# A four-block transformer stack on one core: 768-column rows in block 4, a shared bank in linear attention, loads as a part, tiles reused at the end

## The chip, the core and the metric

The kernel runs on one core of one Trainium2 chip. The time is the device time of one execution, in microseconds. Before the change three runs gave a median of 2755.65 us (2754.45 to 2756.18). One further execution was recorded by the hardware profiler; it took 2750.45 us, and its instructions span 2748.6 us. All durations below are from that execution.

## The reference

The input `x` holds 8 sequences of 1024 rows of 256 numbers in fp32. Four blocks follow each other, each added to `x` and each behind a layernorm without gain (`ln` below):

```
x = x + decoder(ln(x))        # block 1: linear "flow" attention, 16 heads of 16, then
                              #   h = LN1(in + attn @ Wo + bo); LN2(h + gelu(h W1 + b1) W2 + b2), hidden 1024
x = x + relu(ln(x) w1 + b1) w2 + b2          # block 2: hidden 1024
x = x + softmax(q k^T / 16) v                # block 3: one head of 256, per sequence of 1024
x = x + fp4(silu(fp4(y) Wg^T) * (fp4(y) Wu^T)) Wd^T,  y = ln(x)   # block 4: hidden 704
```

In block 1 `q` and `k` are sigmoids; running sums over the rows of `q`, `k` and weighted `q`, `k` give for each row and head a scale for the query and one for the value, and `out = q_scaled @ cumsum(k^T v_scaled)`. In block 4 `fp4` quantises and restores blocks of 16 numbers along a row, for activations and for the weights (whose restored values are written `fp4(W)` in the reference).

## The kernel before

**Tiling.** Work goes by chunks of 128 rows (64 in all), and in block 1 by groups of four chunks (512 rows, 16 groups). TensorE products are fp32; each product in the code is two passes in the trace. Three producers run at once. `linear_attention` does block 1's attention group by group: `front` (load, layernorm, transpose) for four chunks, the q and k products, running sums on VectorE (`prod`), `head_sums`, a trip of a small table through HBM that spreads it over partitions (`packed`, `spread`), the same once more, and then `linear_chunk` four times: values, scores `k q` in 32-row tiles with masks (`sc`), the values product in 32-column tiles that also reads the carried state `kv_sum`, the state's increment `k^T v`, and the output product. `dense` does the two hidden-1024 layers in halves of a group and streams their weights (`w_ff`, five buffers, 128 KB loads) through the one DMA queue of SyncE. `softmax_and_fp4` starts `soft_chunk` for one chunk after another: scores against the whole sequence, exponentials, transposes, value product, then block 4. Two more parts, `fp4_weights` and `softmax_weights`, prepare weights at the start: the first loads the raw weights of block 4 (`w_raw`), quantises them with `fp4` on VectorE and ScalarE and transposes them; the second forms the product of the block-3 query and key weights from `wqk_raw`.

**Order.** The order of the instructions on each engine is fixed when the program is built. `Plan` runs the parts as generators. Each `yield` names an engine, the tiles that must be done, free buffers and PSUM banks, and a priority `at`. `Plan.run` (line 231) picks the part that can start first, and among those the one with the lowest `at`; `took` (line 140) adds an estimated duration for each instruction. The estimates decide the order only; on the chip each engine takes its instructions in that order and waits for what they need. All five engines are pinned to it, and DMAs are all issued by SyncE.

**Buffers.** `TILES` (line 42) gives each kind of working tile a number of buffers. `lin` has 5 (linear attention), `flow` 9, `soft` 5 and `prob` 7 (softmax and block 4), `rows` 4, `x` 4 and `hid` 3 rows of 704 columns. A chunk of block 3 and 4 starts only while fewer than 4 are unfinished, and its first product only while fewer than 2 wait for their values. PSUM has eight banks; `linear_chunk` takes one for the values product and another for `k^T v`.

**Start.** The constants (`rpos`, `same`, `front` among them) are computed on VectorE before anything else, and all biases, gains and small weights are loaded on the SyncE queue before the parts run: x for four chunks, the q, k, v weights, Wo and nine rows spread over the partitions, 128 KB each.

**The end of block 4.** A row of `hid` has 704 = 5 x 128 + 64 columns. `soft_chunk` transposes it tile by tile, copies five full tiles and one of 64 rows to `hqT`, and multiplies six tiles with `wdT`:

```
for k, (f0, rows_) in enumerate(INTER_TILES):
    nc.tensor.matmul(
        bank[:, :D],
        lhsT=hqT[k // 4][:rows_, k % 4, :],
        rhs=wdT[:rows_, k, :],
```

Of the kernel before, what the change touches and what calls it, by code (L numbers as in the profile page):

```python
# [33 lines left out]
BANKS = 8  # L34
INTER_TILES = [(t * P, min(P, INTER - t * P)) for t in range((INTER + P - 1) // P)]
# [9 lines left out]
    "lin": (5, D, F32),  # L45
# [7 lines left out]
    "hid": (3, INTER, F32),  # L53
    "q_c": (2, INTER, BF16),
}


class Plan:
# [9 lines left out]
    def __init__(self, tc, nc):  # L68
        self.tc, self.nc = tc, nc
        self.free = {}  # L70
        self.done = {}
        self.by = {}
        self.banks = []
        self.live = {}
        self.slots = {}
        self.kind = {}
        self.used = {}
        self.held = set()
        self.kept = set()
        self.last = {}  # L80
        self.act_set = 0
        self.parts = []
        for name in ("tensor", "vector", "scalar", "gpsimd", "sync"):
            setattr(self, name, Queue(self, name))
# [19 lines left out]
    def take(self, kind, tile_):  # L104
        name = tile_.tensor.name
        slots, live = self.slots.setdefault(kind, []), self.live.setdefault(kind, set())
        if len(live) + len(slots) == TILES[kind][0]:
# [11 lines left out]

    def slot_free(self, kind):  # L120
        slots, live = self.slots.get(kind, []), self.live.get(kind, ())
        if len(live) + len(slots) < TILES[kind][0]:
            return 0.0
        return min(slots) if slots else None

# [5 lines left out]

    def bank_free(self, tag, n, count):
        banks = self.banks.get(tag, [])
        if len(banks) + count <= n:
            return 0.0
        times = sorted(self.used[b] for b in banks if b not in self.held)
        k = count - (n - len(banks)) - 1
        return times[k] if k < len(times) else float("inf")

    def took(self, queue, op, args, kw):  # L140
# [12 lines left out]
        if queue == "tensor":  # L153
# [4 lines left out]
            if op == "matmul" and (kw["lhsT"].shape[-1] <= 32 or kw["lhsT"].shape[0] <= 32):  # L158
                cost *= 0.25
            after = 0.2  # L160
        elif queue == "vector":
            each = {"reciprocal": 6.2e-3, "tensor_tensor_scan": 2.15e-3}.get(op, 1.05e-3)
            cost = 0.15 + each * size
        elif queue == "scalar":
            cost = 0.2 + 0.95e-3 * size
# [4 lines left out]
        elif queue == "gpsimd":  # L170
            cost = 0.4 + 1.3e-3 * size
        else:
            cost, after = 0.4, 2.2
# [7 lines left out]
        end = start + cost  # L181
        self.free[queue] = end
# [11 lines left out]
    def need(queue, tiles, banks=0, when=None, at=None, unused=(), fresh=None):  # L194
# [3 lines left out]
            queue=queue, tiles=tiles, banks=banks, when=when, at=at, unused=unused, fresh=fresh  # L198
# [14 lines left out]
    def ready(self, need):  # L213
# [8 lines left out]
        if need.fresh is not None:  # L222
            times.append(self.slot_free(need.fresh))
# [7 lines left out]
    def run(self):  # L231
        while self.parts:
            now = self.free.get("tensor", 0.0)
            best = None
            for part in self.parts:
# [3 lines left out]
                key = max(t - now, 0.0), part[1].queue == "tensor", part[2]  # L239
                if best is None or key < best[0]:  # L240
                    best = key, part
            assert best is not None, "every part waits for another"
            if best[0][0] > 0.0:
                self.free["tensor"] = now + best[0][0]
# [42 lines left out]
def block_stack_kernel(ctx: ExitStack, tc: tile.TileContext, a: dict, out: bass.AP):  # L287
# [51 lines left out]
    def make(kind, name=None):  # L339
        bufs, width, dtype = TILES[kind]  # L340
        t = wk.tile([P, width], dtype, tag=kind, name=name or kind, bufs=bufs)
# [11 lines left out]
    def load_row(name, width):  # L353
        t = const.tile([P, width], F32, tag=f"b_{name}", name=f"b_{name}")
        nc.sync.dma_start(out=t, in_=a[name].partition_broadcast(P))
        return t

    def load_tiles(name, width, kt):
        t = const.tile([P, kt, width], F32, tag=f"w_{name}", name=f"w_{name}")
        nc.sync.dma_start(out=t, in_=a[name].rearrange("(k p) n -> p k n", p=P))  # L360
        return t

    def load_cols(name, n):
        t = const.tile([P, n], F32, tag=f"c_{name}", name=f"c_{name}")
        nc.sync.dma_start(out=t, in_=a[name])
        return t
# [32 lines left out]
    for g in range(NG):  # L399
        nc.vector.tensor_scalar(rpos[:, g, :], pos, float(g * GT), None, ALU.add)  # L400
    nc.vector.reciprocal(rpos, rpos)
# [16 lines left out]
    nc.vector.tensor_reduce(  # L418
        same[:, 0, :], ident.rearrange("p (t r) -> p r t", r=32), AX.X, ALU.add
    )  # L420
    front = const.tile([P, G, 32], F32, name="front")
    nc.vector.memset(front, 0.0)
    for t in range(1, G):
        nc.vector.tensor_copy(same[:, t, :], same[:, 0, :])
        nc.vector.tensor_copy(front[: 32 * t, t, :], same[: 32 * t, 0, :])
# [3 lines left out]
    for i in range(V_PADS):  # L429
        v = const.tile([P, H, 32], F32, name=f"v_pad{i}")  # L430
        nc.gpsimd.memset(v, 0.0)
        v_pads.append(v)

# [11 lines left out]
    for i, n in enumerate("qkv"):  # L445
        nc.sync.dma_start(
            out=wqkv[:, :, i * D : (i + 1) * D],
            in_=a[f"L0_attn_W{n}"].rearrange("(k p) n -> p k n", p=P),
        )
        if n != "v":  # L450
# [4 lines left out]
    bv1 = load_row("L0_attn_bv", D)  # L455
    wo = load_tiles("L0_attn_Wo", D, 2)
    bo = load_row("L0_attn_bo", D)
    ln1g, ln1b = load_row("L0_attn_ln1_g", D), load_row("L0_attn_ln1_b", D)
    b1 = load_cols("L0_attn_b1", NF)
    b2 = load_row("L0_attn_b2", D)  # L460
    ln2g, ln2b = load_row("L0_attn_ln2_g", D), load_row("L0_attn_ln2_b", D)
    fb1 = load_cols("L0_ffn_b1", NF)
    fb2 = load_row("L0_ffn_b2", D)
    wv3 = const.tile([P, 2, D], F32, name="wv3")
    nc.sync.dma_start(
        out=wv3, in_=a["L1_attn_W_qkv"][:, 2 * D :].rearrange("(k p) n -> p k n", p=P)
    )
    bsm = load_cols("L1_attn_b_qk", 4)
    bsv = load_row("L1_attn_b_v", D)
# [4 lines left out]
    wdT = const.tile([P, len(INTER_TILES), D], F32, name="wdT")  # L474

# [88 lines left out]
    def fp4_weights():  # L564
# [15 lines left out]
        for i, (src, turns) in enumerate(pieces):  # L580
            for j in range(i, min(i + 3, len(pieces))):
                if j not in raws:
                    ahead = pieces[j][0]
                    raws[j] = (yield from fresh("soft", dma(), "w_raw"))[
# [835 lines left out]
```

## Time and profile before

| | |
|---|---|
| median of 3 runs | 2755.65 us |
| profiled execution | 2750.45 us, span 2748.6 us |
| TensorE (PE) busy | 2614.9 us, 95% |
| TensorE weight loads (PEld) busy | 1998.1 us, 73% |
| VectorE (DVE) busy | 1953.3 us, 71% |
| ScalarE (ACT) busy | 1219.6 us, 44%, of it 285 activation table loads of 1.28 us |
| GpSimd (POOL) busy | 597.7 us, 22% |
| DMA | 211.61 MB, mean 77 GB/s |
| granted TensorE clock, mean | 0.984 |

A row of a group reads: line, engine, operation, output and inputs by name, shape of the tile in the array (rows*columns), operand shape, count, then busy time in us and the mean of one in ns, then the idle time of the engine just before these instructions with what ended it. As passes overlap, the mean of one is longer than the distance from one start to the next. A row of a timeline reads: start, duration, engine, operation and names; PEld is the load of weights into the array, SPq the issue of a DMA. Nearly all rows carry line 268, since one helper issues every instruction, so they are told apart by the names of their tiles. A waiting row reads: total us, times, longest.

### The profile page before, as it was taken

Reading aid. Unit: us, or ns where it says so; the run is one execution under the profiler, and the core shown is the slowest. Engines: PE = TensorE matmul, PEld = TensorE weight load, DVE = VectorE, ACT = ScalarE, POOL = GpSimd, SP = SyncE. Lnnn points to the kernel's source line nnn. Section 1 sums busy time; section 2 is a strip of 40 time slices with the busy share of each in tenths; the row PEclk is TensorE's granted clock in tenths of the full one; section 3 lists DMA queues with packets and bytes.
Section 4 is the critical chain, followed back from the end, with each engine's and each line's share of the span. In section 5 each row is a group of like instructions: output and inputs, shape, how many; then the busy total and the mean of one; then the engine's idle time right before and its main releaser. Section 6 shows DMA issues by size and latency. Waiting matters only on the chain.

```text
span 2748.6 us, 45646 instructions
## 1 busy us (share of the span) xinstructions
PE 2614.9 (95%) x16620; PEld 1998.1 (73%) x16620; DVE 1953.3 (71%) x4459; ACT 1219.6 (44%) x2453; POOL 597.7 (22%) x1100
## 2 busy tenths in 40 slices
PE   3888999999999999999999999999999999999997
PEld 1667677777777777777777777777777777877664
DVE  6877676685867778587776858768685777755565
ACT  2424344534554454444535354444545445353343
POOL 1323322121321312122221223213131222211000
PEclk7999999999999999999999999999999999999999
DMA  4234231322223232232222223222322313122000
GB/s 107 76 103 141 71 104 57 93 71 86 82 68 98 65 92 67 75 102 62 90 66 78 82 79 100 62 90 69 90 65 80 109 49 91 60 80 76 14 12 14
DMA packets 283215, 211.61 MB, mean 77 GB/s; under 512 B 23921, under 2 KB 270705, under 8 KB 282993
## 3 DMA queue, kind: packets, MB, share of 16 engines
q1 hardware_dynamic: 282992, 208.71, 25.5%
q8 instruction: 133, 2.18, 0.3%
q14 instruction: 90, 0.73, 0.1%
HBM read 189.74 MB, written 18.87 MB: 76 GB/s over the span
## 4 chain that ended last, share of the span: by engine, by line
PE 83%; DVE 11%; DMA 2%; ACT 2%; issue 1%; POOL 1%; SPq 0%; DVEq 0%; POOLq 0%; ACTq 0%
PE bank L268 83%; DVE hid L268 3%; DVE n L268 1%; DVE x_amax L268 1%; DVE ln_st L268 1%; DMA spread<-packed 1%; DVE mx L268 1%; DVE sc L268 1%; DVE prod L268 1%; ACT L268 1%; DMA w_ff<-in_L_ffn_w_dram 1%; SPq L268 0%; DVE u L268 0%; DVE x_r L268 0%; POOL ln_rstd L268 0%
## 5 line engine op out<-in xcount | busy, mean ns | idle before, releaser
L268 PE MATMUL bank<-half,w_ff 128*128 128x256 f32 x2048 | 533.8, 384 | 17.1 <-DMA w_ff<-in_L_ffn_w_dram 13.7
L268 PE MATMUL bank<-w_ff,hidden 128*128 128x256 f32 x2048 | 530.4, 384 | 3.4 <-ACT hidden L268 3.4
L268 PEld LDWEIGHTS bank<-half,w_ff 128*128 128x128 f32 x2048 | 382.8, 192 | 94.9 <-issue 32.3
L268 PEld LDWEIGHTS bank<-w_ff,hidden 128*128 128x128 f32 x2048 | 366.9, 191 | 76.4 <-issue 29.6
L268 ACT ACT_TABLE_LOAD x285 | 365.7, 1283 | 61.9 <-PE bank L268 54.6
L268 POOL TENSOR_SCALAR ln_ve<-ln_mv 128x1 f32<-128x1 f32 x384 | 102.4, 267 | 1110.1 <-DVE ln_mv L268 1099.6
L268 ACT ACTIVATE hidden<-bank,c_L_ffn_b 128x256 f32<-128x256 f32 x256 | 120.8, 472 | 320.5 <-PE bank L268 319.8
L268 PE MATMUL bank<-n2T,qT 128*128 128x512 f32 x512 | 243.9, 599 | 2.3 <-ACT qT L268 2.3
L268 POOL TENSOR_TENSOR ln_rstd<-ln_ve,neghalf 128x1 f32<-128x1 f32 x384 | 237.4, 618 | 32.0
L268 PE MATMUL bank<-vt,probT 128*128 128x256 f32 x1024 | 232.2, 380 | 0.0
L268 DVE TENSOR_TENSOR hid<-hid,bank 128x352 f32<-128x352 f32 x128 | 65.9, 518 | 229.4 <-PE bank L268 189.2
L268 PEld LDWEIGHTS bank<-vt,probT 128*128 128x128 f32 x1024 | 194.0, 190 | 38.1 <-issue 7.7
L268 DVE TENSOR_TENSOR sc<-bank,triu 128x512 f32<-128x512 f32 x256 | 162.3, 682 | 54.9 <-PE bank L268 54.9
L268 PE MATMUL bank<-wdT,hqT 128*128 128x256 f32 (+1 forms) x768 | 190.9, 390 | 0.8 <-ACT hqT L268 0.8
L268 ACT ACTIVATE hidden<-bank,c_L_attn_b 128x256 f32<-128x256 f32 x256 | 121.5, 474 | 146.3 <-PE bank L268 144.8
L268 POOL TENSOR_TENSOR xr<-xr,b_L_attn_ln_b 128x256 f32<-128x256 f32 x64 | 62.6, 996 | 531.3 <-DMA xr<-in_L_attn_inputs_dram 531.1
L268 PE MATMUL bank<-wgT,xqT 128*128 128x352 f32 x512 | 175.4, 465 | 1.4 <-ACT xqT L268 1.4
L268 PE MATMUL bank<-wuT,xqT 128*128 128x352 f32 x512 | 172.4, 459 | 0.0
L268 PEld LDWEIGHTS bank<-wdT,hqT 128*128 128x128 f32 (+1 forms) x768 | 139.7, 190 | 40.8 <-issue 20.2
L268 PEld LDWEIGHTS bank<-n2T,qT 128*128 128x128 f32 x512 | 92.7, 191 | 73.7 <-issue 62.5
L268 PEld LDWEIGHTS bank<-wuT,xqT 128*128 128x128 f32 x512 | 97.3, 190 | 54.1
L268 ACT ACTIVATE hid<-bank 128x352 f32<-128x352 f32 x128 | 59.3, 463 | 154.0 <-PE bank L268 152.6
(174 smaller groups left out, 4382.5 us busy)
## 6 DMA issues: line engine op xcount, KB each, us to landing
w_ff<-in_L_attn_W_dram SPq DMA_DIRECT2D x512, 128.0 KB
w_ff<-in_L_ffn_w_dram SPq DMA_DIRECT2D x512, 128.0 KB
spread<-packed SPq DMA_DIRECT2D x96, 256.0 KB
x<-in_L_attn_inputs_dram SPq DMA_DIRECT2D x64, 128.0 KB
xr<-in_L_attn_inputs_dram SPq DMA_DIRECT2D x64, 128.0 KB
rows<-res SPq DMA_DIRECT2D x64, 128.0 KB
rows<-rows SPq DMA_DIRECT2D x64, 128.0 KB
out_dram<-y SPq DMA_DIRECT2D x64, 128.0 KB
```

Source lines behind the costliest of these rows:

```text
L268: ins = method(*args, **kw)
```

## The change

- Block 4's rows are 768 wide. Three `hid` tiles are allocated once, with columns 704 to 767 set to zero, and so are the missing 64 rows of `wdT`. Transposes, the copy and the down product then use full 128-row tiles. The quantisation still covers 704 columns.
- In `linear_chunk`, the values product and `k^T v` share one bank; `start=False` for the second. `lin` has 4 buffers.
- Constants needed later (`rpos`, `same`, `front`) and most loads become parts, `late_constants` and `late_loads`, with priorities of their own; whoever reads them waits for a label in `late`. The preparation of the block-4 weights gets later priorities.
- When the last linear chunk is done, `plan.spare` lets `prob`, `soft` and `rows` also take `flow`, `lin` and `x` tiles, the tiles of `q` and `k` become two more `hid` rows, eight chunks may be unfinished in place of four, and three may wait for values in place of two.
- The planner's estimates change: TensorE pays 0.2 us when the array's shape changes, and a part that stays in 32-wide tiles is preferred; other constants for VectorE, ScalarE and GpSimd; a DMA takes its bytes at 160 GB/s, one behind another, and lands 1.8 us after.

```diff
-    "lin": (5, D, F32),
+    "lin": (4, D, F32),
-    "hid": (3, INTER, F32),
+    "hid": (3, INTER_PAD, F32),
+SPARE = {"prob": "flow", "soft": "lin", "rows": "x"}
...
+            tiled = op == "matmul" and (kw["lhsT"].shape[-1] <= 32 or kw["lhsT"].shape[0] <= 32)
+            if tiled:
                 cost *= 0.25
+            if tiled != self.tiled:
+                cost += 0.2
...
+            if op == "tensor_scalar" and outs[0].dtype == BF16:
+                cost = 0.16 + 0.26e-3 * size
         elif queue == "scalar":
-            cost = 0.2 + 0.95e-3 * size
+            cost = (0.16 if op == "copy" else 0.26) + 0.82e-3 * size
...
         elif queue == "gpsimd":
-            cost = 0.4 + 1.3e-3 * size
+            cost = 0.2 if op == "tensor_scalar" else 0.55 + 0.7e-3 * size
         else:
-            cost, after = 0.4, 2.2
+            cost = 0.4
...
+        if queue == "sync":
+            n = 4e-6 / 160e-3
+            for d in outs[0].shape:
+                n *= d
+            self.free["rings"] = max(self.free.get("rings", 0.0), end) + n
+            after = self.free["rings"] - end + 1.8
...
-                key = max(t - now, 0.0), part[1].queue == "tensor", part[2]
+                stays = self.tiled and part[1].tiled
+                wait = max(t - now - (0.3 if stays else 0.0), 0.0)
+                key = wait, part[1].queue == "tensor", not stays, part[2]
...
+    def late_loads():
+        loads.sort(key=lambda x: x[0])
+        for i, (at, label, t, src) in enumerate(loads):
+            yield dma(at=at)
+            nc.sync.dma_start(out=t, in_=src)
+            if all(x[1] != label for x in loads[i + 1 :]):
+                late.add(label)
...
-    for g in range(NG):
-        nc.vector.tensor_scalar(rpos[:, g, :], pos, float(g * GT), None, ALU.add)
-    nc.vector.reciprocal(rpos, rpos)
...
+    def late_constants():
+        yield dve(at=0.1)
+        for g in range(NG):
+            nc.vector.tensor_scalar(rpos[:, g, :], pos, float(g * GT), None, ALU.add)
+        nc.vector.reciprocal(rpos, rpos)
+        yield dve(at=0.12)
...
+    hids = []
+    for i in range(TILES["hid"][0]):
+        h = const.tile([P, INTER_PAD], F32, name=f"hid{i}")
+        nc.gpsimd.memset(h[:, INTER:], 0.0)
+        hids.append(h)
...
-            at = 0.2 + 2.5 * i / len(pieces)
+            at = 0.9 + 2.2 * i / len(pieces)
...
-        bank = mm_bank()[:, :D]
+        both = mm_bank()
+        plan.keep(both)
+        bank = both[:, :D]
...
-            kvbank = mm_bank()[:, :64].rearrange("p (k d) -> p k d", k=2)
+            kvbank = both[:, D : D + 64].rearrange("p (k d) -> p k d", k=2)
...
-                        start=k == 0,
+                        start=False,
...
+        yield pe(when=lambda: count["linear"] == B * NCH)
+        plan.spare = True
+        for n in ("q", "k"):
+            h = kept([P, 2, GT], n, 1).rearrange("p k t -> p (k t)")
+            nc.gpsimd.memset(h[:, INTER:INTER_PAD], 0.0)
+            hids.append(h[:, :INTER_PAD])
+        plan.size["hid"] += 2
...
-        yield pe(banks=1, when=lambda: count["asked"] == cc and count["asked"] - count["valued"] < 2)
+            and count["asked"] - count["valued"] < (3 if plan.spare else 2),
...
-            bank = tr_bank()
-            for k, (f0, rows_) in enumerate(tiles):
-                nc.tensor.transpose(bank[:rows_, k, :], hid[:, f0 : f0 + rows_], ident)
+            bank = turned([hid[:, f0 : f0 + P] for f0, _ in tiles])
...
+            nc.scalar.copy(hqT[half][:, : len(tiles), :], bank)
...
-                lhsT=hqT[k // 4][:rows_, k % 4, :],
-                rhs=wdT[:rows_, k, :],
+                lhsT=hqT[k // 4][:, k % 4, :],
+                rhs=wdT[:, k, :],
...
-                when=lambda: q["normed"] == NCH and cc - count["out"] < 4 and "softmax" in weights,
+                when=lambda: q["normed"] == NCH and cc - count["out"] < (8 if plan.spare else 4) and "softmax" in weights,
...
-    for part in (linear_attention(), dense(), softmax_and_fp4(), fp4_weights(), softmax_weights()):
+    for part in (linear_attention(), late_constants(), late_loads(), dense(), softmax_and_fp4(), fp4_weights(), softmax_weights()):
```

## The prediction

> **What bounds the kernel now.** I read the page's busy shares first, then the four stretches of the run by busy time, then the waits of TensorE, then the groups split by shape, and last the timelines of one block-4 product and of the first 46 us.
>
> ```profile
> PE 2614.9 (95%) x16620; PEld 1998.1 (73%) x16620; DVE 1953.3 (71%) x4459; ACT 1219.6 (44%) x2453; POOL 597.7 (22%) x1100
> ```
>
> TensorE is busy for 2614.9 of 2748.6 us, so 133.7 us are idle. The stretches (from:to, length, then busy time by engine, granted clock) show where:
>
> ```profile
> 0.00:100.00 100.00, 44.80 (x441) 30.54 (x445) 66.90 (x168) 22.36 (x58) 16.98 (x43) 0.81 0.31 83
> 100.00:420.00 320.00, 288.66 (x2041) 228.37 (x2037) 241.42 (x553) 131.79 (x285) 91.72 (x165) 0.95 0.36 106
> 420.00:2550.00 2130.00, 2116.23 (x13479) 1626.33 (x13468) 1525.68 (x3472) 991.99 (x1960) 479.90 (x875) 1.00 0.26 79
> 2550.00:2748.60 198.60, 165.18 (x681) 112.91 (x679) 119.26 (x267) 73.47 (x151) 9.07 (x18) 0.96 0.04 12
> ```
>
> Idle on TensorE: 55.2, 31.3, 13.8 and 33.4 us. For 2130 us it is the bound with nothing to spare, so there only less TensorE time counts. In the first 420 us and the last 200 us it waits for others; there an earlier start or more chunks in flight count.
>
> The longest waits of TensorE, totals over the run with count and longest, are of those two ends, and no engine starves it in between:
>
> ```profile
> PE bank L268 <- DVE prod L268: 20.7, 6, 7.8
> PE bank L268 <- DVE n L268: 16.6, 9, 11.3
> PE bank L268 <- DVE hid L268: 14.4, 5, 7.3
> PE bank L268 <- DMA w_ff<-in_L_ffn_w_dram: 13.7, 2, 7.2
> PE bank L268 <- DMA wqk_raw<-in_L_attn_W_qkv_dram: 8.4, 1, 8.4
> ```
>
> **Block 4 padded to 768 columns.** The last of six tiles of the down projection has 64 rows. By shape (count, busy, mean ns):
>
> ```profile
> L268 PE MATMUL bank<-wdT,hqT 128*128 128x256 f32 x640 | 150.8, 383 | 0.8 <-ACT hqT L268 0.8
> L268 PE MATMUL bank<-wdT,hqT 64*128 64x256 f32 x128 | 44.5, 428 | 0.0
> ```
>
> And one product in the steady part, with the rows of another that show the weight loads:
>
> ```profile
> 1320.24 2.02 PEld L268 LDWEIGHTS bank<-wdT,hqT 128*128 128x128 f32 x10 [0.20 <-issue]
> 1322.60 0.29 PEld L268 LDWEIGHTS bank<-wdT,hqT 64*128 64x128 f32 x2 [0.33 <-issue]
> 1323.22 0.89 PEld L268 LDWEIGHTS bank<-wgT,xqT 128*128 128x128 f32 x4 [0.33 <-issue]
> ...
> 1325.69 3.62 PE L268 MATMUL bank<-vt,probT 128*128 128x256 f32 x16
> 1329.15 1.05 PE L268 MATMUL bank<-wgT,xqT 128*128 128x352 f32 x3
> ...
> 1347.68 2.95 PE L268 MATMUL bank<-wdT,hqT 128*128 128x256 f32 x12
> 1350.56 0.44 PE L268 MATMUL bank<-ident,n 128*128 128x128 f32 x2
> ```
>
> The weight load stands idle for 0.33 us before the 64-row tile and again before the next full one: it is not overlapped with the product ahead. Sixteen full passes take 1329.15-1325.69 = 3.46 us, 0.216 each; twelve of them would take 2.59. The product takes 1350.56-1347.68 = 2.88. So 0.29 us a chunk x 64 chunks = **-18.4 us**, nearly all where TensorE is the bound. The page "TensorEngine Tiling (Array Packing)" of the Trainium skill speaks against this: its tables (Theoretical Speedup; Row Tiling) recommend a 64-row tile for a contraction of 64, with up to twice the rate. By that, the two last passes would take half of 2 x 0.216 now, and padding would lose 0.22 x 64 = 14 us. The row decides: the two passes lie alone between full tiles, with no second 64-row tile beside them, and pay both changes of shape. The transpose of the last 64 columns already streams 128 columns and stays. ScalarE writes one copy in place of two (about 0.15 us x 64): nothing, it is 44% busy. GpSimd gains four small memsets before its first layernorm work, under 1 us by its 0.52 us for a 512-column memset, hidden by VectorE, which gets to the normalisation later.
>
> **Order of tiled products.** The planner now charges a change of array shape and keeps 32-wide products together. Counted in the two instruction orders, changes fall from 294 to 280. A change costs about 0.09 us (the passes of 0.216 take 0.31 at a change): **-1.3**.
>
> **Late loads and constants.** Before, the first transposes run at 11.3 but the third normalisation is stuck on VectorE behind the quantisation of a block-4 weight that lands at 18.4, and TensorE's second half of the transposes behind W_qk:
>
> ```profile
> 18.42 0.42 DVE L268 TENSOR_REDUCE x_amax<-w_raw 128x16 f32<-128x256 f32 x1 [6.72 <-DMA w_raw<-in_L_ffn_w_gate_dram]
> 20.88 0.69 PE L268 MATMUL bank<-ident,wqk_raw 128*128 128x128 f32 x2 [8.44 <-DMA wqk_raw<-in_L_attn_W_qkv_dram]
> 33.85 1.22 DVE L268 TENSOR_TENSOR_SCAN prod<-one,k 128x512 f32<-128x512 f32 x1
> ```
>
> In the new order all four normalisations, then all transposes, then the first q/k products precede W_qk; rpos, same and front (about 4 us) move between and behind the statistics. But one weight's first four VectorE steps still stand before the first scan. Its transfer is the queue's 3072nd KB both before (x 512, four 256 KB weights, nine 128 KB rows, wv 256, itself 128) and after (x, the four weights, five rows, W_qk 512, one w_ff 256, itself). It lands at 18.4 again; four steps take 1.5 us, and the scan starts at 20.0 instead of 33.85. Its input is there by then: without rpos, same and front ahead of them the statistics start near 5.6, the four normalisations end near 13.0 (x and W_k, the queue's first 1024 KB, have landed by 8), and the first q/k product takes 3.3 us on the slow clock (23.49 to 26.79 before) and the sigmoid 0.7, so k is ready near 18. Without the weight in front the scan would gain 2 us more. The scan chain, the two trips through HBM (packed, spread) and the four chunks follow in nearly the same order, so the first dense product moves from 98.1 by 13.9. The queue behind it holds another 2560 KB, at 3072 KB in about 15.5 us until 31.3; the first packed row is sent at about 31.5, so 1 us may be lost: **-13** (bounds -5 and -18). The loads put behind W_qk and w_ff (norms, wv, its bias) have landed by 31.3 and are first read beyond 100 in the old run, near 90 in the new: the gap of some 55 us covers them; without it each 128 KB row would cost 0.6. Late next is the 256 KB spread of each flow.
>
> **Better costs of transfers and engines.** In 100 to 420 us the two waits for w_ff (13.7) follow a w_ff load issued behind 1 MB of spread. The planner now counts such backlog and may put other work there, but little other work exists yet. Between 0 and all of it, and 8 us the other way since the earlier start asks for weights sooner: I take **-6**.
>
> **One bank for values and k v.** VectorE's read of k v must now follow ScalarE's copy of xo, as the new waits show; before, 90.35 (kv) overlaps 90.18 (xo). The page "PSUM — Partial Sum Buffer" (PSUM bank collisions) asks for this guard by bank. Queued behind it on VectorE are the masks of the next scores. Uncovered it would cost a copy, 0.37 us x 56 = 20.7; by the rows the delay is 0.2 to 0.37 and the next reader of the sum has over 3.5 us of TensorE work before it. Only the first group has no cover: **+1**. One bank less in demand and one fewer `lin` tile (4, not 5): nothing; the new order leaves more TensorE work between scores and their use (lower quartile 5 to 6.4 us against 4.6 to 5).
>
> **Tiles reused for the last chunks.** Work on TensorE behind the last wv product is 146 us in both orders; before, this took 194. Behind the last qT product lie 26.4 us of work before (it took 47) and 35.0 after: 8.6 of idle filled. Of the other 17.8 us of idle since 2550 I take half, since eight chunks with three at the scores leave other work at each wait: **-17** (bounds -5, -26). The clock of 0.96 over 165 us of work costs 6.6; half goes: **-3**.
>
> **Sum.** -18.4-1.3-13-6+1-17-3 = -57.7 on the profiled execution's 2750.45 (span 2748.6 and 1.9 around it): 2692.7. The median of the runs lies 5.2 above that execution: **2698**.
>
> **Rivals.**
> - The early gain is taken back by the stalls in 100 to 420 us, since weights are asked for sooner and the transfers are no faster: +19, 2717. For: w_ff waits there already. Against: the chain of the second group moves forward too.
> - The tail stays bound by the latency of a chunk, its quantisation on VectorE (7.3 us wait in the last): only -3 of the -20, 2715. For: VectorE steps are the same. Against: idle is spread over many chunks.
> - More: early stalls down by 13 more and the tail by 10 more, 2675.
> - Slower: VectorE, waiting for xo behind an activation table load (1.28) and a hidden activation (0.47) on ScalarE, lets scores pile up and TensorE stall in each chunk: 1.75 x 56 = 98, 2796. It decides from 57.7/56 = 1.03 us a chunk. Against: 13.8 us idle in 2130, and 29% free on VectorE.
> - The new order does nothing net, about 2755: the planner's other choices cost what the steps gain. Nothing in the profile asks for it.
>
> **How the numbers follow.** All as stated 0.50 (own range 2685 to 2712), early gain lost 0.18, tail kept 0.15, more 0.09, same 0.03, slower 0.05. A run tells from no change what exceeds 0.2% (5.5 us). Faster 0.92, same 0.03, slower 0.05. Range 2672 to 2730: from the better case to past both partial losses.
>
> **What would show it.** Right: no 64-row group and 2.6 us a product; first scan near 20, first dense product near 85; idle after the last dense product under 20 us, clock there above 0.97; 420 to 2550 idle still under 1%. Wrong: waits for kv or w_ff growing, idle of the steady part above 30 us, or a first scan still past 30.

## The result

The changed kernel takes 2736.28 us (median of five runs, 2731.74 to 2747.50) against 2755.65 us before: a ratio of 0.994, with a 95% interval of 0.9922 to 0.9957. It is faster, by 19 us. The forecast was 2698 us, 58 us faster, and its range began at 2672 and ended at 2730, so the measured time lies outside. The direction was right and the size was not.

The profiled execution of the changed kernel took 2747.50 us, the longest of the five; a likely reason stands in the last section. TensorE's share on its page has hardly moved:

```profile
PE 2608.8 (95%) x16620; PEld 2010.2 (73%) x16620; DVE 1960.9 (71%) x4459; ACT 1212.5 (44%) x2389; POOL 573.7 (21%) x1106
```

The same stretches as before (length, busy time of PE, PEld, DVE, ACT and POOL, granted clock, DMA share, GB/s), changed kernel:

```profile
0.00:100.00 100.00, 57.44 (x523) 39.25 (x524) 77.73 (x187) 30.47 (x71) 27.85 (x64) 0.85 0.32 91
100.00:420.00 320.00, 298.88 (x2218) 232.83 (x2217) 251.12 (x582) 128.96 (x288) 88.57 (x162) 0.97 0.36 104
420.00:2550.00 2130.00, 2084.01 (x13172) 1617.38 (x13171) 1508.30 (x3414) 982.24 (x1890) 446.14 (x858) 0.99 0.26 78
2550.00:2745.80 195.80, 168.48 (x711) 120.74 (x709) 123.71 (x278) 70.84 (x141) 11.16 (x22) 0.95 0.05 14
```

In the first 420 us TensorE is busy for 356.3 us; it was 333.5 before. The new kernel is 23 us ahead there. Between 420 and 2550 us the idle time has grown from 13.8 to 46.0 us, and the clock has come off 1.00. That stretch (the steady part below) had been the one with nothing to lose. The waits of TensorE there (from 420 to 2550 us; total, times, longest) have new names. First the longest of the changed kernel, then those of the kernel before:

```profile
PE bank L297 <- DVE n L297: 9.7, 10, 2.5
PE bank L297 <- DVE prod L297: 7.7, 4, 2.0
PE bank L297 <- DMA w_ff<-in_L_ffn_w_dram: 7.5, 4, 2.4
PE bank L297 <- issue: 5.9, 6, 1.5
```

```profile
PE bank L268 <- DVE u L268: 3.7, 6, 0.6
PE bank L268 <- ACT hidden L268: 3.4, 6, 0.6
PE bank L268 <- ACT half L268: 2.8, 6, 0.5
```

("issue" is time in which TensorE waited for nothing that the profile shows.) Before, no wait in this stretch was for `w_ff` or `prod`, and none reached 1.0 us. Now sixteen waits of 1.0 to 2.5 us, spread over the stretch, make 29 of the 46 us. Over the whole run, waits for `w_ff` rose from 2 to 9.

### The profile page after: what moved, and what is told of

Its sections match the earlier page's. It is cut to its first block, busy times and chain, and to the rows that moved or that the text cites. A ratio compares the mean times of both kernels' runs of the same rounds, so it can differ in the third digit from the quotient of the medians.

```text
span 2745.8 us, 45511 instructions
## 1 busy us (share of the span) xinstructions
PE 2608.8 (95%) x16620; PEld 2010.2 (73%) x16620; DVE 1960.9 (71%) x4459; ACT 1212.5 (44%) x2389; POOL 573.7 (21%) x1106
## 3 DMA queue, kind: packets, MB, share of 16 engines
q1 hardware_dynamic: 282992, 208.71, 25.8%
## 4 chain that ended last, share of the span: by engine, by line
PE 66%; DVE 23%; DMA 3%; issue 3%; ACT 3%; POOL 2%; SPq 0%; DVEq 0%; ACTq 0%; POOLq 0%
PE bank L297 66%; DVE hid L297 4%; DVE n L297 3%; DVE prod L297 2%; DVE ln_st L297 2%; DVE x_amax L297 2%; POOL ln_rstd L297 1%; DVE u L297 1%; DMA spread<-packed 1%; DVE mx L297 1%; ACT q_c L297 1%; DVE x_r L297 1%; DVE ln_mv L297 1%; DVE spread L297 1%; DVE res L297 1%
## 5 line engine op out<-in xcount | busy, mean ns | idle before, releaser
L297 POOL TENSOR_SCALAR ln_ve<-ln_mv 128x1 f32<-128x1 f32 x384 | 96.1, 250 | 1471.8 <-DVE ln_mv L297 1461.6
L297 PE MATMUL bank<-wdT,hqT 128*128 128x256 f32 x768 | 180.3, 385 | 1.0 <-ACT hqT L297 1.0
L297 PEld LDWEIGHTS bank<-wdT,hqT 128*128 128x128 f32 x768 | 147.7, 193 | 23.3 <-ACT hqT L297 2.4
L297 PE MATMUL bank<-ident,n 128*128 128x128 f32 x512 | 98.1, 280 | 35.5 <-DVE n L297 32.2
L297 PEld LDWEIGHTS bank<-wgT,xqT 128*128 128x128 f32 x512 | 95.6, 193 | 42.2 <-issue 8.9
```

What stands on the lines that cost most here:

```text
L297: ins = method(*args, **kw)
```

## The experiments

All times are medians; the kernel before, run beside them on the same chip, gave 2752.7 to 2756.7. The first question was whether the full tiles bring what the sum said, and whether the planner's new estimates or the new buffers bring the idle time.

### 1. Full tiles alone

The sixth tile starts 64 columns earlier and overlaps the fifth; the weight rows that meet the repeated columns are zero.

```diff
-                nc.tensor.transpose(bank[:rows_, k, :], hid[:, f0 : f0 + rows_], ident)
+                nc.tensor.transpose(bank[:, k, :], hid[:, f0 + rows_ - P : f0 + rows_], ident)
...
-                lhsT=hqT[k // 4][:rows_, k % 4, :],
-                rhs=wdT[:rows_, k, :],
+                lhsT=hqT[k // 4][:, k % 4, :],
+                rhs=wdT[:, k, :],
```

> The kernel before, its instruction order kept, with one edit: the sixth tile of block 4 covers columns 576 to 703 in place of 640 to 703, and the weight rows that meet the 64 repeated columns are zero, so all six tiles have 128 rows and no buffer grows. Theory A (the row-shape price of 0.29 us a chunk is real and lies on TensorE): 18 us less than before, about 2737. Rival (the gap of the 64-row tile was covered, or full tiles pay elsewhere): within 6 us of before, 2750 to 2756.

Measured: 2738.22 us, ratio 0.9939 (0.9924 to 0.9954), 16 us less. The group by shape, and one product in the timeline of this run:

```profile
L268 PE MATMUL bank<-wdT,hqT 128*128 128x256 f32 x768 | 178.6, 382 | 0.8 <-ACT hqT L268 0.8
```

```profile
1343.30 2.75 PE L268 MATMUL bank<-wdT,hqT 128*128 128x256 f32 x12
1345.89 0.38 PE L268 MATMUL bank<-ident,n 128*128 128x128 f32 x2
```

The twelve passes take 1345.89-1343.30 = 2.59 us; they took 2.88. Theory A holds, and it needs no wider row: no buffer grows for the overlapping tile. This single edit gives nearly what the whole change gives. So the other parts together bring about 2 us more, although the first 420 us gained 23.

### 2. The old planner under the new parts

The planner's `took` and `run` are put back as they were before, the transfer estimate included.

```diff
-                stays = self.tiled and part[1].tiled
-                wait = max(t - now - (0.3 if stays else 0.0), 0.0)
-                key = wait, part[1].queue == "tensor", not stays, part[2]
+                key = max(t - now, 0.0), part[1].queue == "tensor", part[2]
...
```

> The change with the planner's old estimates and its old rule of choice put back; padding, shared bank, four lin tiles, late loads and tiles reused at the end stay. Theory A (the new estimates write an order that stalls TensorE between 420 and 2550 us): idle there falls from 46 to under 20 us and the time to 2700 to 2712. Rival B (fewer lin tiles or the shared bank cause these stalls): idle there stays above 35 us and the time at 2730 to 2742.

Measured: 2743.92 us. Idle between 420 and 2550 us is 30.0, between the two expectations, and the first dense product is at 96.7 us in place of 85.0. Neither theory as written: the old planner stalls less in the steady part, but loses the start.

### 3. No reuse of tiles at the end

```diff
-        plan.spare = True
```

(with the two added `hid` rows.)

> The change without the reuse of tiles at the end: four chunks unfinished, two waiting for values, as before. If the reuse is worth what the two profiles show after 2550 us (8 us): 2744 and idle after 2550 near 33 us. If it is worth nothing: 2736.

Measured: 2740.47 us, 4 us more than the whole change and between the two expectations. The five runs of the whole change alone spread over 16 us, so 4 is a rough figure; it is far from the 20 in the prediction.

### 4. The old transfer estimate

```diff
-            self.free["rings"] = max(self.free.get("rings", 0.0), end) + n
-            after = self.free["rings"] - end + 1.8
+            after = 2.2
```

> The change with one estimate put back: a transfer is again taken to land 2.2 us after its issue, without a count of the bytes ahead of it. If the new transfer estimate is what brings the w_ff stalls between 420 and 2550 us: these (8 us) go and the time is 2722 to 2728. If the other estimates do it: 2733 to 2740. If the estimate was helping: above 2742.

Measured: 2798.41 us, ratio 1.0158 (1.0141 to 1.0175): 62 us slower than the whole change. The first dense product is back at 98.2 us, and 58.6 us are idle between 420 and 2550 us. Counting the bytes ahead of a transfer helps, and it is also what gives the early start: late loads without it, here and in the second experiment, gain at most 1.3 us at the first dense product. The 62 us are the price in this surrounding: between the second kernel and the seventeenth below (2715.70 us), which differ in this estimate and in GpSimd's, it is 28.

### 5 to 7. One suspect each, taken out of the whole change

```diff
# 5: no charge for a change of shape, no preference
-                stays = self.tiled and part[1].tiled
+                stays = False
...
# 6: five lin tiles, rows of 704 columns with the overlapping sixth tile
-    "lin": (4, D, F32),
+    "lin": (5, D, F32),
...
# 7: a bank of its own for k v
-            kvbank = both[:, D : D + 64].rearrange("p (k d) -> p k d", k=2)
+            kvbank = mm_bank()[:, :64].rearrange("p (k d) -> p k d", k=2)
...
```

> The change without the planner's charge for a change of the array's shape and without its preference (and 0.3 us of allowed wait) for parts that stay in 32-wide tiles. Theory C (the preference puts tiled parts ahead of what is due, so weights, running sums and normalisations come late between 420 and 2550 us): idle there from 46 to about 20 us, time 2705 to 2715. Rival D (buffers: four lin tiles, a shared bank): idle there stays near 45, time 2733 to 2742, plus 1 us for more changes of shape.

> The change with five lin tiles again; the room comes from hid rows of 704 columns, whose sixth tile covers columns 576 to 703 against weight rows of which the first 64 are zero, so all tiles still have 128 rows. Rival D: idle between 420 and 2550 us falls from 46 to about 30 us (what the old estimates left), time 2718 to 2726. Theory C: no change beyond 5 us, 2731 to 2741.

> The change with k v in a bank of its own again. If VectorE's wait for the copy of xo costs time: 2724 to 2731, and fewer waits for prod and n. If it is hidden, as the prediction took it: within 5 us of 2736.

Measured: 2739.24, 2738.56 and 2737.20 us, with 39.0, 40.8 and 39.7 us idle in the steady part. None helps. An order planned anew also moves a little whatever the edit, so differences of a few microseconds between such runs are not read here as effects. Taking suspects out one at a time from the whole did not find the loss; building up from the kernel before did.

### 8. Three parts only

Full tiles (overlapping), late loads and constants with the later priorities of the block-4 weights, and the transfer estimate; all else as before.

```diff
+            self.free["rings"] = max(self.free.get("rings", 0.0), end) + n
+            after = self.free["rings"] - end + 1.8
...
+    for part in (linear_attention(), late_constants(), late_loads(), dense(), softmax_and_fp4(), fp4_weights(), softmax_weights()):
```

> The kernel before with three parts of the change only: full tiles in block 4 (by the overlapping sixth tile), late loads and constants, and the transfer estimate that counts bytes. Five lin tiles, two banks, old estimates for the engines, no preference for tiled parts, no reuse at the end. If the early gain (19 us at 420 us) and the full tiles (16 us) add up and nothing is lost in between: 2718 to 2722. If the steady part always takes back what the start gains: 2733 to 2740.

Measured: 2712.93 us, ratio 0.9843 (0.9825 to 0.9862), faster than both kernels. Idle time between 420 and 2550 us is 25.8 us. The gains do add up when the rest stays out, and to more than the 2718 to 2722 that was expected.

### 9 and 10. The engine estimates, with the reuse at the end

The tenth adds the reuse of tiles to the eighth. The ninth is the tenth with the new estimates for VectorE, ScalarE and GpSimd.

```diff
+            if op == "tensor_scalar" and outs[0].dtype == BF16:
+                cost = 0.16 + 0.26e-3 * size
-            cost = 0.2 + 0.95e-3 * size
+            cost = (0.16 if op == "copy" else 0.26) + 0.82e-3 * size
-            cost = 0.4 + 1.3e-3 * size
+            cost = 0.2 if op == "tensor_scalar" else 0.55 + 0.7e-3 * size
```

> The kernel of the eighth experiment (full tiles, late loads and constants, the transfer estimate) with the reuse of tiles at the end, the new estimates for VectorE, ScalarE and GpSimd, and nothing else. Theory E (the tighter engine estimates leave the order without slack): idle between 420 and 2550 us back above 35 us and the time at 2730 to 2740. Rival F (no single estimate does it; the tiled preference, the planner's clock rule and the buffers each cost a share): 2710 to 2722.

> The kernel of the eighth experiment with the reuse of tiles at the end added (eight chunks unfinished, three waiting for values). If the reuse helps where the rest is in order: 2700 to 2709. If the end is bound by the latency of the last chunk: 2710 to 2716.

Measured: 2758.22 us with the new estimates, ratio 1.0015 (1.0006 to 1.0024), and 2708.50 without, ratio 0.9833 (0.9816 to 0.9851). Three lines of estimates, which change no instruction and only their order, cost 50 us here, as much as the start, the full tiles and the reuse bring together. The stretch from 420 to 2550 us, first the ninth run, then the tenth:

```profile
420.00:2550.00 2130.00, 2083.47 (x13161) 1613.30 (x13160) 1506.60 (x3406) 989.74 (x1892) 458.29 (x856) 1.00 0.26 78
```

```profile
420.00:2550.00 2130.00, 2103.08 (x13389) 1638.08 (x13382) 1530.20 (x3480) 1031.40 (x1944) 465.33 (x869) 1.00 0.26 78
```

In this stretch the ninth has 46.5 us idle against 26.9, as theory E expected, and its time lies past the range of theory E. Idle time is not all of it. The busy times of the whole run, the ninth and then the tenth, for the same 16620 passes:

```profile
PE 2615.2 (95%) x16620; PEld 2010.5 (73%) x16620; DVE 1959.8 (71%) x4459; ACT 1217.5 (44%) x2391; POOL 583.9 (21%) x1101
```

```profile
PE 2596.5 (96%) x16620; PEld 2007.6 (74%) x16620; DVE 1953.5 (72%) x4459; ACT 1251.9 (46%) x2415; POOL 582.9 (22%) x1101
```

The spans are 2759.5 and 2709.1 us. Of the 50 us between them 32 are idle time of TensorE and 19 are busy time; the mean clock (0.985 and 0.986) accounts for about 4 of these 19, and the rest was not traced further. The reuse itself gives 4 us (2712.93 to 2708.50), as in the third experiment, again less than the spread of the runs (2707.75 to 2717.23 in the eighth).

### 11 and 12. The preference for tiled parts, and the buffers

The eleventh is the eighth with the charge and the preference. The twelfth is the eighth with four `lin` tiles and the shared bank.

```diff
# 11
+            if tiled != self.tiled:
+                cost += 0.2
...
+                stays = self.tiled and part[1].tiled
# 12
+    "lin": (4, D, F32),
...
+            kvbank = both[:, D : D + 64].rearrange("p (k d) -> p k d", k=2)
```

> The kernel of the eighth experiment with the charge for a change of the array's shape and the preference for 32-wide tiles added. If the preference is what costs in the steady part: 2728 to 2738, idle there above 35 us. If not: 2708 to 2716.

> The kernel of the eighth experiment with four lin tiles and the shared bank for values and k v. If these buffers cost time once nothing else is in the way: 2722 to 2735. If they are free, as the prediction took them: 2708 to 2717.

Measured: 2720.85 and 2709.24 us. The preference costs 8 us here, between the two expectations, with 33.6 us idle from 420 to 2550 us against 25.8; it was forecast to gain 1.3. Four tiles and one bank are free here: 3.7 us less than the eighth, which is within what a new order moves.

### 13 to 15. Which estimate

The tenth with one new estimate each: VectorE's bf16 step, ScalarE's line, GpSimd's line of the diff above.

> The kernel of the tenth experiment (2708.5) with the new estimate for VectorE alone: a tensor_scalar with bf16 output 0.16 us + 0.26 ns a column (0.34 at 704 columns) in place of 0.15 + 1.05 ns (0.89). Theory E1 (this 0.55 us was the slack of each block-4 chunk in the order; without it, normalised rows and hid come late): 2735 to 2755. Rival E2 (it is ScalarE's or GpSimd's): 2705 to 2714.

> The kernel of the tenth experiment with the new estimate for ScalarE alone (a 256-column copy 0.37 in place of 0.44, an activation of 256 columns 0.47 in place of 0.44, of 512 columns 0.68 in place of 0.69). Theory E1: 2705 to 2714. If ScalarE's estimate is the cause: 2735 to 2755.

> The kernel of the tenth experiment with the new estimate for GpSimd alone (the two steps of a layernorm's reciprocal root 0.20 and 0.55 in place of 0.40 and 0.40; 256 columns 0.73 both times). Theory E1: 2705 to 2714. If GpSimd's estimate is the cause: 2735 to 2755.

Measured: 2740.31, 2736.16 and 2702.72 us, with 42.3, 40.1 and 25.4 us idle from 420 to 2550 us (26.9 in the tenth). Two estimates do it, VectorE's (+32) and ScalarE's (+28); their sum is above the 50 of the ninth, so they overlap. Theory E1 had named one. GpSimd's does not cost: with it this is the lowest median of the study, ratio 0.9819 (0.9802 to 0.9836), an interval that overlaps the tenth's. As its order differs from the tenth's too, from the first 25 us on, a new order does not cost time merely by being new. The waits of TensorE over the whole run, first of the tenth run, then of the thirteenth, show what comes late with VectorE's shorter step:

```profile
PE bank L293 <- ACT prob L293: 9.8, 11, 1.9
PE bank L293 <- DMA w_ff<-in_L_ffn_w_dram: 4.0, 1, 4.0
```

```profile
PE bank L295 <- ACT prob L295: 25.3, 25, 2.3
PE bank L295 <- DMA w_ff<-in_L_ffn_w_dram: 9.5, 10, 1.6
```

The exponentials of block 3 and the weights of the dense layers, neither of which is a VectorE step, keep TensorE waiting more often. In the fourteenth run the names are others again (`v`, a VectorE result, 12 times between 420 and 2550 us, `half` 12 times), so no single wait carries the loss.

### 16 and 17. Putting estimates back in the whole change

The sixteenth is the whole change with the three engine estimates put back. The seventeenth keeps GpSimd's, puts back VectorE's and ScalarE's, and also takes out the preference with its charge, and the planner's new clock rule. This rule is a part of the change that the list above leaves out: it moves the planner's TensorE time on to the moment at which the chosen TensorE part is ready. By the code it differs from the old rule only where the preference has forgiven a wait of up to 0.3 us; without the preference both rules give the same time. So it is no cause of its own, and three edits are put back, not four.

```diff
# 17, besides the engine lines
-            if best[0][0] > 0.0 or best[1][1].queue == "tensor":
-                self.free["tensor"] = max(now, best[2])
+            if best[0][0] > 0.0:
+                self.free["tensor"] = now + best[0][0]
```

> The whole change, only the estimates for VectorE, ScalarE and GpSimd put back. If they are what the change lost, also with all else in place: 2708 to 2722. If the tiled preference, the clock rule or the buffers keep it slow: 2728 to 2738.

> The whole change with the estimates for VectorE and ScalarE, the tiled preference and the planner's clock rule put back; padding to 768, shared bank, four lin tiles, late loads, reuse at the end, the transfer estimate and GpSimd's estimate stay. If these four edits of the planner are all that the change lost: 2700 to 2710. If the padding's memory and the buffers cost more together: above 2716.

Measured: 2728.69 us and 2715.70 us. In the whole change the engine estimates alone account for 8 us (the intervals, 0.9894 to 0.9936 and 0.9922 to 0.9957 for the whole change, overlap), and with the preference for 21, which is clear of noise (0.9841 to 0.9874). The 50 us of the ninth run is the price in one surrounding, not a constant; and the preference, whose removal alone gained nothing (experiment 5), is worth 13 us once the estimates are back, together with GpSimd's new estimate, in which the two kernels differ too.

The seventeenth lies between its two expectations. What still separates it from the fifteenth, at 2702.72 us, are the rows of 768 columns in place of the overlapping tile, the shared bank and the four `lin` tiles, and nothing else: 13 us (10 by the ratios to the kernel before), with intervals that do not overlap. Tiles and bank cost nothing in the twelfth run, and giving each back to the whole change gained nothing in experiments 6 and 7. Which of the three costs here was not tested.

### 18. Longer estimates

The tenth with VectorE's and ScalarE's new estimates, each 15% longer.

```diff
+        if queue in ("vector", "scalar"):
+            cost *= 1.15
```

> The kernel of the tenth experiment with the new estimates for VectorE and ScalarE, each made 15% longer. If the old estimates were good because they were long (slack in the order, not their accuracy): 2700 to 2718. If it is where the slack lies (the bf16 step, the 512-column activations), and not how much: 2728 to 2750.

Measured: 2733.75 us. Making the new estimates longer in proportion does not bring back the 2708.5, as the second expectation had it. It leaves VectorE's bf16 step at 0.39 us, far from the 0.89 of the old estimate, so slack at this one step is not ruled out. Why the old pair gives the better order is left open.

## Why the prediction was wrong, point by point

**The step that failed.** "Better costs of transfers and engines" was costed in the first 420 us alone, and the new order between 420 and 2550 us at nothing. The working there was a count that scores have more TensorE work behind them; it looked at one pair of producer and consumer and took it for the order. The runs show that this stretch has a price: 46.0 us idle in place of 13.8. In the seventeenth experiment three edits of the planner (the estimates for VectorE and ScalarE, and the preference with its charge) are worth 2736.3-2715.7 = 21 us of the 38 that are missing; added to the tenth kernel, each of the two estimates alone costs about 30. Even the order with late loads that has the least idle time there, 24.5 us in the twelfth run, is above the 1% that was expected. The prediction's own sign of being wrong, idle above 30 us and more waits for `w_ff`, is what came. Its rivals held this only for a single mechanism, the wait for `xo` behind VectorE, and at 0.05. The one called "nothing net" named the right cause, choices of the planner that cost what the steps gain, and dismissed it as something that the profile does not ask for. No profile of the kernel before could ask for it: the order did not exist there.

**The second step: the end of the run, mis-sized.** -20 was forecast (-17 and -3 for the clock); the third experiment gives 4, the tenth against the eighth 4. That is some 16 us more. That 21 and 16 nearly make up the 38 is in part luck: the parts were measured in different surroundings, the first 420 us of the fifteenth run gain 27 us where 19 were forecast, and with that the fifteenth kernel comes within 5 us of the forecast although its end, 185.2 us behind the last `wv` product, is no shorter. From the last `wv` product to the end, before and after:

```profile
2554.10:2748.60 194.50, 161.32 (x664) 110.13 (x662) 117.16 (x263) 72.36 (x148) 9.07 (x18) 0.96 0.04 12
```

```profile
2561.20:2745.80 184.60, 157.74 (x665) 112.60 (x663) 115.63 (x259) 67.90 (x135) 9.69 (x18) 0.95 0.04 13
```

The end did shorten, by 10 us. The first experiment has 3 of these from full tiles (191.2 us), and the third, without the reuse, has 186.1 us, so no more than 2 come from the reuse there and the rest from the new order; between the eighth and the tenth it is 4.5 (193.9 to 189.4). What was taken as filled was not. From the last `qT` product to the end, before and after:

```profile
2701.60:2748.60 47.00, 31.22 (x124) 20.81 (x122) 25.27 (x49) 12.94 (x27) 0.74 (x2) 0.93 0.03 9
```

```profile
2689.30:2745.80 56.50, 42.15 (x162) 31.11 (x160) 31.35 (x68) 12.49 (x26) 2.13 (x4) 0.87 0.03 10
```

More work lies behind this product, but it lengthens the end in place of filling it: 15.8 us idle became 14.4, where 8.6 were to be filled. The clock gave nothing back (0.96 to 0.95 behind the last `wv` product).

**Full tiles, -18.4: right,** 16 us by the first experiment, with the row (2.88 to 2.59 us a product) as read. The row was the better guide: the rule of the Trainium skill that it was weighed against, "TensorEngine Tiling (Array Packing)" (Theoretical Speedup; Row Tiling), would have made it a loss, as the prediction read it for a lone tile.

**Late loads and constants, -13: right in size, for one wrong reason.** Rows of VectorE's and TensorE's timelines of the changed kernel:

```profile
16.11 0.42 DVE L297 TENSOR_REDUCE x_amax<-w_raw 128x16 f32<-128x256 f32 x1 [0.61 <-DMA w_raw<-in_L_ffn_w_gate_dram]
21.35 1.23 DVE L297 TENSOR_TENSOR_SCAN prod<-one,k 128x512 f32<-128x512 f32 x1 [3.80 <-ACT k L297]
```

```profile
16.81 5.90 PE L297 MATMUL bank<-n0T,wqkv 128*128 128x512 f32 x8 [0.46 <-ACT n0T L297]
85.04 1.03 PE L297 MATMUL bank<-half,w_ff 128*128 128x256 f32 x4
```

The first dense product moved from 98.07 to 85.04, by 13.0 us. That the figure is met so exactly is luck: with the same loads it came at 83.3 us in the eighth run and at 87.0 in the tenth, which share one order of VectorE's instructions up to 2370 us. The first scan came at 21.35 (forecast 20.0), held up by `k` and not by the weight, which landed at 16.1 and not at 18.4: the q and k products started at 16.8, not at 14. And the gain depends on the transfer estimate (experiments 2 and 4), which the sum had put in another step.

**The stalls from 100 to 420 us, -6: right in kind.** Idle there fell by 10 us, from 31.3 to 21.1.

**Shared bank and four `lin` tiles, +1 and nothing: right where it was tested.** The twelfth run has both and is not slower, and the seventh, with a bank of its own, gains nothing. The guard by bank that the Trainium skill asks for ("PSUM — Partial Sum Buffer", PSUM bank collisions) shows on VectorE in the changed kernel, whose `kv` now waits for ScalarE's copy:

```profile
DVE kv L297 <- ACT xo L297: 11.2, 14, 2.9
```

TensorE does not pay for it: one wait of 0.2 us in the whole run names `kv`. The 13 us between the fifteenth and the seventeenth kernel, which differ in these two parts and the wider rows, stay open.

**Order of tiled products, -1.3: wrong in sign.** The preference cost 8 us in the eleventh run and, by the sixteenth and seventeenth, up to 13 in the whole change. It did not even save changes of shape in the eleventh: by the start times in the traces, TensorE changes between 32-wide and full tiles 238 times in the eighth run and 252 times in the eleventh. That it costs by putting back other work is argued, not shown.

## What to carry to other kernels

A change to a planner's estimates is a change to everything that is planned, even where the new numbers are nearer to the trace (VectorE's bf16 step of 704 columns takes 0.35 us in the profile of the kernel before; the new estimate is 0.34, the old one 0.89); cost the steady part too, or change one estimate at a time: with the old ones for VectorE and ScalarE and without the preference, 2708.5 and 2702.7 us were reached here against 2736.3. Where TensorE is saturated, look for a lone partial tile between full ones: padding it, or letting it overlap its neighbour against zero weights, removed the price of two changes of shape here, 0.29 us each time; the overlap needs no wider row. When removing parts one by one from a changed kernel shows nothing, add them one by one to the kernel before.

## What the runs showed that was not expected

The kernel before repeated within 2753 to 2757 us in its five runs, the changed one only within 2732 to 2748. Five runs are few: beside the experiments the kernel before itself spread from 2746.9 to 2761.3. A part of the changed kernel's spread can be seen in its trace all the same. Most of its waits of about two microseconds are followed by half the clock. One such wait in the timeline of the changed kernel, and then steps of 3.41 us around it and around two waits without this effect, at 528 and 1677 us (after the five busy times: the granted clock):

```profile
1857.64 2.04 PE L297 MATMUL bank<-half,w_ff 128*128 128x256 f32 x4 [2.43 <-DMA w_ff<-in_L_ffn_w_dram]
```

```profile
1854.24:1857.65 3.41, 0.98 (x6) 0.56 (x4) 3.20 (x10) 0.36 (x1) 2.15 (x5) 1.00 1.09 240
1857.65:1861.06 3.41, 3.41 (x10) 2.85 (x11) 3.34 (x9) 0.97 (x2) 1.62 (x2) 0.50 0.21 61
1861.06:1864.48 3.42, 3.42 (x20) 2.93 (x20) 2.43 (x8) 1.53 (x6) 1.05 (x4) 1.00 0.26 77
523.04:526.45 3.41, 2.79 (x11) 1.35 (x10) 3.31 (x6) 0.59 (x1) 0.00 (x0) 1.00 1.07 195
526.45:529.87 3.42, 1.77 (x8) 1.59 (x9) 3.28 (x7) 0.52 (x2) 0.00 (x0) 1.00 0.59 150
529.87:533.28 3.41, 3.41 (x18) 2.89 (x16) 3.25 (x7) 1.24 (x1) 0.00 (x0) 1.00 0.00 0
1673.33:1676.75 3.42, 1.79 (x28) 1.14 (x28) 3.31 (x7) 1.76 (x2) 0.00 (x0) 1.00 0.02 7
1676.75:1680.16 3.41, 3.20 (x19) 2.26 (x20) 3.27 (x10) 0.55 (x3) 0.74 (x2) 1.00 0.13 37
```

The four passes after the wait take 2.04 us in place of 1.03. In the clock record of this trace every half-clock stretch begins and ends on one grid with steps of 3.413 us; the rows above are steps of it. Between 420 and 2550 us seven steps ran at half the clock. They cost 1.7 us each, 12 us together that no idle time shows; before, there was none. This stretch has nine waits of 1.8 us or more, and seven were followed by such a step. The grid tells them apart: in this stretch each step with 1.82 us idle or more was followed by half the clock, and no step with 1.65 or less was. The waits at 528 and 1677 us lie across an edge, which leaves 1.65 and 1.63 us in their fuller steps. In the other traces the border is less clean: a step with 1.72 us idle (fourth run) was followed by half the clock, one with 1.94 (ninth run) was not. The Trainium skill ("TensorE: Matmul & The Clock Gate", Part 1: The HAM clock gate) gives a free-running window of about 3.4 us and has the clock fall after at least one idle window; the length agrees with this trace, but here 1.82 to 2.54 us idle within one step were enough. The profiled execution had a mean clock of 0.984 over 2745.8 us, the other four 0.986 to 0.987 over 2730.0 to 2736.5; that where the waits fall on this grid makes a part of the spread from run to run is likely by these numbers, but was not tested by itself.
